# Splitting one 1x1 convolution's third output tile over two banks of the attention buffer

## The chip, the cores and the metric

The kernel runs on one core of a Trainium2 chip. The metric is the time of one execution on the device in microseconds (us), taken as the median of several executions. TensorE (PE in the profile) multiplies matrices, VectorE (DVE) and ScalarE (ACT) work elementwise and empty the matmul results, GpSimd (POOL) does copies, and DMA queues (SP) move data. Matmul results land in PSUM, which is divided into eight banks[...].

## What is computed

The input is eight images of 384 channels and 64x64 pixels. Two layers follow each other, each with a residual:

```python
x = x + L0(gn(x))   # windowed attention: norm, qkv, two branches of 4 heads, 8x8 windows, projection
x = x + L1(gn(x))   # 1x1 conv, a filter on 8x8 patches in the frequency domain,
                    # 3x3 depthwise conv, gate, 1x1 conv:
    x1, x2 = t[:, :192], t[:, 192:]
    g = gelu(x1) * x2
    return einsum('bchw,oc->bohw', g, w_out)
```

The change is in the last line. The weight `w_out` is 384 x 192: the sum runs over 192 gated channels, the result has 384 channels, and the residual is added to it.

## The kernel before

An image is cut into eight strips of eight pixel rows, 512 tokens each. Channels lie on partitions in three tiles of 128. For each image a strip passes through attention, is added to the input and written to DRAM, and is later read back for the second layer.

The work is written as small pieces (`qk_tile`, `scores`, `weights`, `back`, `finish` and so on). Each is given a place on one time line with `at(place, piece, ...)`, and the pieces are emitted in the order of their places. All matmuls and transposes go through the helpers `matmul` (L53) and `transpose` (L56), which keep TensorE's instructions in exactly this order. The order on the other engines is settled by the framework's scheduler when the kernel is built. The second layer of image b runs between the attention pieces of image b+1; only the last image's second layer has no attention beside it.

The eight PSUM banks are dealt out to two pools. `psum` gives one of four single banks (tag "gemm"). `psum2` gives one of two double banks (tag "att"), used in turn by the attention pieces: `scores` writes pS, `turn` pT, `apply` pA, `put` po. In the last image's second layer `conv_taps` uses them too (pc). A buffer is handed to the next tile only when the last reader of the tile before it is done.

The readers that matter here are on VectorE. `normalise` reads pA with a reciprocal (L483) and one multiplication of 128x768 (L484); `weights` reads pS with additions of the position bias (L436). The depthwise convolution's taps (L653) are on VectorE too; their first operand zz comes from ScalarE (L647), which works on the strip that ScalarE has just copied out of pz (L609, L612).

The order on TensorE at one `finish`, by the places in the plan (in units of one attention branch), is: `back` of the newest strip (place 1.99 of its cycle), `apply` of the previous branch (1.00), `scores` of the new branch (0.05), `finish` (0.10), the first `qk_tile` of the next branch (0.14), `put` of the previous branch (0.23). `normalise` has place 0.07 of the same unit, but it is VectorE's.

`finish` (its additions are L686) is the last 1x1 convolution of one strip. Its 192 input channels are a full tile g0 of 128 and a tile g1 that holds the other 64 channels twice: both halves of g1's partitions carry the same 64 channels, so that either half of the array can take them. For each of three output tiles pw there are one 128x128 matmul with g0 and two 64x64 matmuls with g1, each over 512 tokens. A 64x64 matmul occupies a quarter of the array, named by the half of its input partitions (`r`) and the half of its output partitions (`half`). There are 64 calls of `finish`: 8 images by 8 strips.

## Time and profile before

The median of three runs is 3776.54 us (3773.02 to 3777.32). The profiled execution took 3771.3 us.

| engine | busy us | share of the span |
|---|---|---|
| TensorE matmul (PE) | 3639.9 | 97% |
| TensorE weight loads (PEld) | 2315.5 | 61% |
| VectorE (DVE) | 2839.3 | 75% |
| ScalarE (ACT) | 2379.7 | 63% |
| GpSimd (POOL) | 438.2 | 12% |

TensorE's granted clock is 0.997 of full speed over the run. The span falls into three parts: loading and preparing up to about 590 us, then image after image with both layers beside each other up to about 3525 us, then the last image's second layer alone.

An fp32 matmul appears in the trace as two records, one for each pass: the 64 x 6 small matmuls of `finish` are 768 records, its 64 x 3 full ones 384. A group's line gives the line, engine, operation, output and inputs, the shape, how many records, their busy time together, the mean duration of one, and the idle time of the engine before them. Matmuls overlap in the pipeline, so the distance between the starts of two records says more than the duration of one.

### The profile page before, as it was taken

What the parts mean: (1) busy time and instruction counts of PE and PEld (TensorE: products, weight loads), DVE (VectorE), ACT (ScalarE), POOL (GpSimd) and SP (SyncE); (2) the same over time, 40 slices, a digit from 0 to 9 for tenths busy, and PEclk for the clock granted to TensorE, in tenths of its full rate; (3) what the DMA queues carried; (4) which work ended last, traced back from release to release, by engine and by line L of the source; (5) the groups of instructions that cost most, each with busy time, mean ns of one, the idle gap of its engine ahead of it and who ended that gap; (6) DMA issues with size and microseconds to landing.
All of it is one profiled execution on the core that took longest, in us unless ns stands there. A gap on an engine that the chain in (4) does not pass through costs nothing.

```text
span 3771.3 us, 88216 instructions
## 1 busy us (share of the span) xinstructions
PE 3639.9 (97%) x38144; PEld 2315.5 (61%) x38144; DVE 2839.3 (75%) x4601; ACT 2379.7 (63%) x3946; POOL 438.2 (12%) x776
## 2 busy tenths in 40 slices
PE   4999999999999999999999999999999999999898
PEld 2666666666666666666666656666666666666554
DVE  4554578777877687777887778877788777777898
ACT  1767676666676576665766756666676666676442
POOL 5111111111101011101101011111011111100000
PEclk9999999999999999999999999999999999999999
DMA  4222222323322233323332322322232222221422
GB/s 120 85 82 74 90 99 99 107 88 108 123 97 82 88 132 107 116 79 115 108 113 83 115 96 99 132 79 99 93 127 99 107 88 82 99 79 71 160 101 76
DMA packets 144488, 377.03 MB, mean 100 GB/s; under 512 B 12308, under 2 KB 12900, under 8 KB 144100
## 3 DMA queue, kind: packets, MB, share of 16 engines
q1 hardware_dynamic: 139952, 370.60, 27.9%
q8 instruction: 300, 4.92, 0.5%
q0 software_dynamic: 2048, 0.15, 0.1%
q10 hardware_dynamic: 2100, 0.63, 0.1%
q14 instruction: 88, 0.72, 0.1%
HBM read 270.54 MB, written 100.79 MB: 98 GB/s over the span
## 4 chain that ended last, share of the span: by engine, by line
PE 86%; DVE 5%; ACT 4%; issue 2%; DMA 2%; POOL 0%; ACTq 0%; DVEq 0%; POOLq 0%
PE pq L53 24%; PE pr L53 13%; PE pt L53 13%; PE pvv L53 12%; PE pw L53 6%; PE pS L53 3%; PE pA L53 3%; PE pz L53 3%; PE pT L56 3%; PE po L56 3%; DVE zz L653 2%; PE pf L53 2%; PE ln L53 2%; PE pc L53 1%; DMA rs<-line 1%
## 5 line engine op out<-in xcount | busy, mean ns | idle before, releaser
L653 DVE SCALAR_TENSOR_TENSOR zz<-z,dw_sb,zz 128x512 f32<-128x512 f32 x1490 | 1106.5, 761 | 189.3 <-ACT zz L647 166.5
L53 PE MATMUL pq<-y,wqk_sb 128*128 128x512 f32 x2160 | 990.3, 596 | 0.1
L53 PEld LDWEIGHTS pq<-y,wqk_sb 128*128 128x128 f32 x2160 | 402.8, 190 | 456.5 <-issue 424.7
L53 PE MATMUL pt<-wi_sb,xn 128*128 128x384 f32 x1536 | 535.2, 486 | 7.2 <-DVE x_finish L686 7.2
L53 PE MATMUL pr<-oT,wp_sb 128*128 128x512 f32 x1152 | 523.1, 592 | 1.0 <-DVE oT L517 1.0
L53 PE MATMUL pvv<-wv_sb,y 128*128 128x192 f32 x2880 | 496.0, 326 | 0.1
L53 PEld LDWEIGHTS pvv<-wv_sb,y 128*128 128x128 f32 x2880 | 471.6, 190 | 36.7 <-issue 23.4
L374 ACT ACTIVATE qab<-pq,bq_sb,cst 96x512 f32<-96x512 f32 (+1 forms) x256 | 198.0, 773 | 398.8 <-PE pq L53 397.1
L53 PEld LDWEIGHTS pt<-wi_sb,xn 128*128 128x128 f32 x1536 | 286.1, 190 | 212.9 <-issue 48.6
L374 ACT ACTIVATE kcd<-pq,vec 32x512 f32<-32x512 f32 x512 | 348.9, 681 | 9.0
L53 PEld LDWEIGHTS pr<-oT,wp_sb 128*128 128x128 f32 x1152 | 211.1, 190 | 224.4 <-issue 211.6
L356 POOL COPY y<-y 128x384 f32<-128x384 f32 x112 | 100.2, 895 | 1608.0 <-PE pvv L53 1108.2
L329 DVE TENSOR_TENSOR lr<-m 128x128 f32<-128x128 f32 x64 | 19.7, 308 | 318.3 <-ACT m L327 318.3
L647 ACT ACTIVATE zz<-z,dw_sb 128x512 f32<-128x512 f32 x183 | 133.9, 733 | 192.5 <-PE pw L53 187.0
L315 POOL TENSOR_TENSOR sq<-sq 128x512 f32<-128x512 f32 x128 | 167.4, 1308 | 634.3 <-ACT sq L313 629.3
L374 ACT ACTIVATE qcd<-pq,bq_sb,cst 96x512 f32<-96x512 f32 (+1 forms) x256 | 197.3, 771 | 43.9 <-PE pq L53 40.6
L526 DVE SCALAR_TENSOR_TENSOR x_add<-pr,vec,x_add 128x512 f32<-128x512 f32 x192 | 143.6, 748 | 105.6 <-PE pr L53 103.8
L564 ACT COPY t<-pt 128x384 f32<-128x384 f32 x256 | 124.9, 488 | 147.8 <-PE pt L53 145.0
L408 ACT COPY v<-pvv 128x384 f32<-128x384 f32 x256 | 121.2, 480 | 130.5 <-PE pvv L53 130.0
L53 PE MATMUL pw<-zz,wo_sb 128*128 128x512 f32 x384 | 181.9, 610 | 0.0
L374 ACT ACTIVATE kab<-pq,vec 96x512 f32<-96x512 f32 (+1 forms) x256 | 174.4, 681 | 9.0 <-PE pq L53 7.4
L449 ACT ACTIVATE e<-e 128x1024 f32<-128x1024 f32 x128 | 135.3, 1057 | 53.4 <-DVE e L443 52.0
(139 smaller groups left out, 5273.0 us busy)
## 6 DMA issues: line engine op xcount, KB each, us to landing
x_add<-in_x_dram SPq DMA_DIRECT2D x64, 768.0 KB
x1d<-x_add SPq DMA_DIRECT2D x64, 768.0 KB
x_mix<-x1d SPq DMA_DIRECT2D x64, 768.0 KB
x_finish<-x1d SPq DMA_DIRECT2D x64, 768.0 KB
out_dram<-x_finish SPq DMA_DIRECT2D x64, 768.0 KB
x_norm<-in_x_dram SPq DMA_DIRECT2D x61, 768.0 KB
x_stats<-in_x_dram SPq DMA_DIRECT2D x56, 768.0 KB
rs<-line SPq DMA_DIRECT2D x62, 256.0 KB
```

Of the source, the lines that this page charges most:

```text
L53: tc.keep_in_program_order(nc.tensor.matmul(*args, **kw))
L56: tc.keep_in_program_order(nc.tensor.transpose(*args, **kw))
L315: nc.gpsimd.tensor_tensor(sq[:, 0, :], sq[:, 0, :], sq[:, k, :], ALU.add)
L329: nc.vector.tensor_tensor(rc, m[:, 0:P], m[:, 0:P], ALU.mult)
L356: nc.gpsimd.tensor_copy(dst[:, :, :, :, 0:4], src[:, :, :, :, 4:8])
L374: return nc.scalar.activation(dst[to:to + n], pq[of:of + n], AF.Identity, bias=bias[of:of + n], scale=scale)
L408: nc.scalar.copy(v[:, 2 * g:2 * g + 2, :, 0:HD], pvv[:, 0:384].rearrange("p (g h d) -> p g h d", g=2, h=4))
L449: nc.scalar.activation(e, e, AF.Exp)
L526: nc.vector.scalar_tensor_tensor(t[:, m, :], pr, bp_sb[:, m:m + 1], t[:, m, :], ALU.add, ALU.add)
L564: nc.scalar.copy(t1, pt[:, 0:C])
L647: nc.scalar.activation(zz.rearrange("p (r c) -> p r c", c=SW), z[:, 1:9, 1:SW + 1], AF.Copy, scale=dw_sb[:, m, 4:5])
L653: i = nc.vector.scalar_tensor_tensor(acc.rearrange("p (r c) -> p r c", c=SW), z[:, dy:dy + 8, dx:dx + SW], dw_sb[:, m, TAPS[tap]:TAPS[tap] ...
```

## The change

Before, the third output tile had its two small matmuls in two of the four quarters, over 512 tokens each. The change cuts this tile by tokens into two halves of 256 and gives it a double bank of the attention pool in place of a single bank: tokens 0 to 255 in the first bank, 256 to 511 in the second. The first half's two small matmuls read input rows 0 to 63, the second half's read rows 64 to 127, so that the four small matmuls of 256 tokens lie in all four quarters. The full matmul of this tile is also cut in two, all small matmuls come ahead of all full ones as before, and the three additions to the residual follow all four full matmuls in the program; the third reads both banks in one instruction.

```diff
-        pw = [psum(f"pw_{b}_{s}_{m}") for m in range(KC)]
-
-        for m, half, r in ((0, 0, 0), (1, 1, 1), (0, 1, 0), (1, 0, 1), (2, 0, 0), (2, 1, 1)):
+        pw = [psum(f"pw_{b}_{s}_{m}") for m in range(2)]
+        pw2 = psum2(f"pw2_{b}_{s}")
+        full, lo, hi = slice(0, ST), slice(0, 256), slice(256, ST)
+        pw = [(pw[0], 0, full), (pw[1], 1, full), (pw2[:, 0, lo], 2, lo), (pw2[:, 1, lo], 2, hi)]
+
+        for i, half, r in ((0, 0, 0), (1, 1, 1), (0, 1, 0), (1, 0, 1), (2, 0, 0), (3, 1, 1), (2, 1, 0), (3, 0, 1)):
+            p, m, tok = pw[i]
             rows, cols = slice(r * 64, (r + 1) * 64), slice(half * 64, (half + 1) * 64)
-            matmul(pw[m][cols], wo_sb[rows, 1, m * P + half * 64:m * P + half * 64 + 64], g1[rows],
+            matmul(p[cols], wo_sb[rows, 1, m * P + half * 64:m * P + half * 64 + 64], g1[rows, tok],
                    start=True, stop=False)
-        for m in range(KC):
-            matmul(pw[m], wo_sb[:, 0, m * P:(m + 1) * P], g0, start=False, stop=True)
-            zs["added"] = nc.vector.tensor_tensor(t[:, m, :], pw[m], t[:, m, :], ALU.add)
+        for p, m, tok in pw:
+            matmul(p, wo_sb[:, 0, m * P:(m + 1) * P], g0[:, tok], start=False, stop=True)
+        for m in range(2):
+            nc.vector.tensor_tensor(t[:, m, :], pw[m][0], t[:, m, :], ALU.add)
+        by_half = t[:, 2, :].rearrange("p (o n) -> p o n", o=2)
+        zs["added"] = nc.vector.tensor_tensor(by_half, pw2[:, :, lo], by_half, ALU.add)
```

## The prediction

> **What bounds the kernel now.** I read the page first. Matmuls are busy for 97% of the span, and the chain that ended last is 86% TensorE's:

> ```profile
> PE 3639.9 (97%) x38144; PEld 2315.5 (61%) x38144; DVE 2839.3 (75%) x4601; ACT 2379.7 (63%) x3946; POOL 438.2 (12%) x776
> ...
> PE 86%; DVE 5%; ACT 4%; issue 2%; DMA 2%; POOL 0%; ACTq 0%; DVEq 0%; POOLq 0%
> ```

> So TensorE's time is nearly the kernel's: a column saved there is time saved, and a wait put into its queue is time lost. The view by stretches gives TensorE 2886.8 us busy in the 2935 us from 590 to 3525 us, thus 48 us idle. The waits of TensorE in that stretch:

> ```profile
> PE pS L53 <- issue: 18.3, 25, 2.0
> PE pT L56 <- ACT e L449: 8.1, 8, 1.5
> PE pt L53 <- DVE x_finish L686: 7.2, 6, 1.4
> PE pz L53 <- ACT v L408: 6.6, 12, 1.0
> PE pA L53 <- issue: 6.2, 8, 2.7
> ```

> (columns: total us, times, longest). None is for pA's reader, the multiplication on L484: TensorE never waits for `normalise` now. The groups that the change touches, over the whole run (records, busy us, mean ns of one | idle before):

> ```profile
> L53 PE MATMUL pw<-zz,wo_sb 128*128 128x512 f32 x384 | 181.9, 610 | 0.0
> ...
> L53 PE MATMUL pw<-g,wo_sb 64*64 64x512 f32 x768 | 130.7, 606 | 6.6 <-DVE g L668 5.1 <-issue 1.4
> ```

> Then I read the timeline around single calls of `finish`. This one, at 1106 us, is typical (start, duration, engine, line, operands, count):

> ```profile
> 1105.22 0.22 PE L53 MATMUL pA<-v,eT 64*64 64x49 f32 x1
> ...
> 1105.68 1.54 DVE L653 SCALAR_TENSOR_TENSOR zz<-z,dw_sb,zz 128x512 f32<-128x512 f32 x2 [3.79 <-ACT zz L647]
> ...
> 1106.16 0.59 PE L53 MATMUL pw<-g,wo_sb 64*64 64x512 f32 x1
> ...
> 1106.17 1.94 PE L53 MATMUL pw<-g,wo_sb 64*64 64x512 f32 x11
> ...
> 1107.14 0.25 DVE L483 RECIPROCAL rc<-pA 128x16 f32<-128x16 f32 x1
> 1107.31 0.70 DVE L653 SCALAR_TENSOR_TENSOR zz<-z,dw_sb,zz 128x512 f32<-128x512 f32 x1
> 1107.92 0.95 DVE L484 TENSOR_TENSOR o<-pA,rc 128x768 f32<-128x768 f32 x1
> 1108.03 2.84 PE L53 MATMUL pw<-zz,wo_sb 128*128 128x512 f32 x6
> ...
> 1109.45 0.68 DVE L436 TENSOR_TENSOR e<-pS,bias 128x512 f32<-128x512 f32 x1
> ...
> 1110.05 0.68 DVE L436 TENSOR_TENSOR e<-pS,bias_odd 128x512 f32<-128x512 f32 x1
> ```

> The reader is to see three things. TensorE goes from pA's last matmul straight through pS to pw. VectorE frees pA only at 1107.92 + 0.95 = 1108.87, after three taps (L653), of which the first was held up by ScalarE's zz (3.79 us idle). pS is freed later still, at 1110.73. At the moment of `finish` both double banks are thus in use.

> [...] the four small matmuls of the first two tiles (eight records) take 0.861 us together, and so do the two of the third tile (four records). [...] the third tile's two matmuls come from different rows into one bank, and start 7 to 140 ns apart. [...] `normalise` stands behind taps that wait for ScalarE.

> **The change, part by part.**

> *Columns removed.* Single records start 429 ns apart at 512 columns, 323 at 384 and 163 at 192, so about 0.84 ns a column and some 216 ns at 256. The third tile's small matmuls take two passes of 429 ns = 0.86 us now, and would take 2 x 0.216 = 0.43 us with all quarters filled. **Saved: 0.43 us a call.** The full matmul cut in two is 4 records of 216 ns for 2 of 429, 6 ns more: nothing. Its additional weight load of 190 ns lies beside passes of 216 ns, as the loads of pvv (190 ns, passes of 163 ns) already do. The 64 calls save 27.5 us at most: 52 of them lie beside attention, where TensorE sets the pace (22.4 us), and 12 in the last image's stretch. There, from 3525 to 3771 us, VectorE is busy for 215 us and TensorE for 219 of 246, so I count half of 5.2, 2.6 us. **Together 25.0 us.**

> *Additions.* Three of 681 ns stay three with as many elements. They now follow the fourth full matmul in the program, but VectorE already does them later than that (1111.31 at the call above, when the full matmuls had ended at about 1110.7), so this costs nothing.

> *The single bank set free.* One of four, sooner. The 7.2 us that pt waits for the additions (L686) should go.

> *The wait added.* pw2 takes a double bank in the middle of pA, pS, po. The one that comes free first is pA's. So the fifth small matmul must wait for L484, whose result TensorE needs only at `put` today, after the full matmuls and a `qk_tile`. Queued behind it on TensorE is everything: the full matmuls, for which ScalarE's zz (L647) and VectorE's additions wait, the `qk_tile`, whose copies ScalarE makes, then po and pT. I worked the wait out for every call beside attention from the timeline: TensorE would be at the third tile 0.861 us after the first small matmul; the bank is free at the end of L484, plus 0.055 us, which is what TensorE takes to start after VectorE's end where it waits for L686 today. For the call shown: 1108.87 + 0.055 - 1107.08 = 1.85 us. Seven calls of the 52 lose nothing, the typical one 1.2 to 1.9, eighteen over 2.1 and the worst 3.9 us. **The sum is 86.4 us**, 1.66 us a call. The bank is free 3.4 us after pA's last matmul (median; 1.3 to 5.9), and TensorE wants it after 1.7 us. The 53rd call, at 3521 us, finds no pS beside it and takes another bank. In the last image's stretch pc is read (3622.9 us) well before the next but one asks (3628 us), so no wait is added.

> *What is taken back.* Where TensorE is held up, the others get ahead of it. pT's wait for the exponentials (8.1 us) and pt's for the additions (7.2) are small lags of VectorE and ScalarE; I take 12 of these 15.3 us as absorbed (bounds 0 and 15.3). po would take pS's bank in place of pA's; L436 ended 0.5 to 4 us before po started in the calls that I read, and po comes later than before. No cost.

> *Sum:* 3776.5 - 25.0 + 86.4 - 12 = **3826 us**, 1.3% slower.

> **The rivals.**

> 1. *The wait in full, nothing absorbed* (chance 0.15). The idle time of TensorE stays as it is, and the last stretch gains nothing: 3776.5 + 86.4 - 22.4 = 3841. For it: most idle time of TensorE is put down to "issue" and not to a lag. Against it: the added waits give every other engine time.
> 2. *The long waits shrink* (0.20). The eighteen calls over 2.1 us are those in which the first tap waited longest for ScalarE. With TensorE held back about 1.2 us net at each call, ScalarE may be less late; if no call waits for more than 1.85 us, the sum is 63.2 us, and the time 3776.5 - 25.0 + 63.2 - 12 = 3803. Against it: ScalarE's lateness grows inside one cycle from pz on, and pz moves with TensorE.
> 3. *No wait: faster* (0.15). VectorE's order is settled anew when the kernel is built. If `normalise` stood ahead of the taps, it would end 1.3 us after pA (the least in the trace), and TensorE asks no sooner than 1.54 us after it. The time would be 3776.5 - 25.0 = 3751. For it: seven calls are free already. Against it: the change gives `normalise` no earlier place, and in the calls around 1106 us the taps fill exactly the time in which pA isn't ready.
> 4. *Half of it* (0.08): some calls reordered, about 3776.5 - 25 + 43 - 12 = 3783.

> **How the numbers follow.** My forecast has 0.42, and its time is the prediction. The cases at 3803, 3826 and 3841 together have 0.77; with the half case 0.85. The range from 3776 to 3848 holds these and leaves out the fast one. Within 0.2% of before (3769 to 3784) lies about half of the half case and a little of the fast one: 0.06. Faster 0.14, slower 0.80.

> **What would show it.** In the profile after: a wait "pw <- DVE o L484" as TensorE's largest, some 45 times and 60 to 90 us; the group pw<-g with 64x256 records at about 216 ns apart, busy time of all pw<-g down by some 25 us; L484 still behind two or three L653; pt's wait for L686 gone, pT's smaller. I would be wrong if L484 stood directly behind pA in VectorE's order, if the third tile's matmuls started at once after the fourth, or if ScalarE's zz (L647), which waits for pw today (187 us), set off a new wait of TensorE behind it.

## The result, and the profile after

The changed kernel takes 3866.09 us (3865.25 to 3868.92), against 3776.81 before: a ratio of 1.024, 95% interval 1.0227 to 1.0253. It is 89 us slower; the forecast was 50 us slower, and the range ended 18 us too low. The profiled execution took 3864.6 us, 93.3 more than before.

Busy time and chain of the page of the changed kernel (the same two lines as shown of before, and the clock's line; each of its digits is the granted TensorE clock in tenths of full speed, 9 for 90% or more, in one of 40 slices):

```profile
PE 3660.4 (95%) x38528; PEld 2353.6 (61%) x38528; DVE 2846.7 (74%) x4601; ACT 2380.4 (62%) x3946; POOL 437.9 (11%) x776
...
PEclk9999999999999999999999999999999999999999
...
PE 65%; DVE 17%; ACT 9%; DMA 5%; issue 3%; POOL 0%; ACTq 0%; DVEq 0%; POOLq 0%; SPq 0%
```

The clock's line shows nothing: a slice is 97 us, too coarse for what follows. The chain that ended last has gone over in part from TensorE (86% before, 65% now) to VectorE and ScalarE (9% before, 26% now): it now runs through the convolution's taps and ScalarE's copies. What connects them with TensorE is the first line of TensorE's waits in the stretch beside attention, 590 to 3610 us:

```profile
PE pw L53 <- DVE o L484: 76.7, 40, 3.7
PE pS L53 <- issue: 19.6, 26, 2.2
PE pz L53 <- ACT v L408: 6.7, 12, 1.0
PE pT L56 <- ACT e L449: 6.3, 6, 1.2
PE pvv L53 <- ACT kcd L374: 5.9, 7, 1.2
```

(Columns: total us, times, longest.) The first line is new. pt's wait for the additions (7.2 us before) is gone, pT's has shrunk from 8.1 to 6.3, and a wait of pvv for kcd has come in. The groups of pw over the whole run, from the page, which takes records of 512 and 256 columns together, and then the small matmuls of 256 columns by themselves:

```profile
L53 PE MATMUL pw<-zz,wo_sb 128*128 128x512 f32 (+1 forms) x512 | 207.7, 554 | 0.0
...
L53 PE MATMUL pw<-g,wo_sb 64*64 64x512 f32 (+1 forms) x1024 | 121.7, 520 | 84.2 <-DVE o L484 76.7
...
L53 PE MATMUL pw<-g,wo_sb 64*64 64x256 f32 x512 | 49.2, 428 | 76.9 <-DVE o L484 76.7
```

The small matmuls cost 121.7 us busy, 9.0 less than before, where the prediction looked for some 25; the full ones 207.7, where before they cost 181.9 for just as many columns. These 25.8 us more for the same columns are what the prediction had no term for. One call shows both effects. This is the timeline of TensorE alone:

```profile
2410.36 1.21 PE L53 MATMUL pw<-g,wo_sb 64*64 64x512 f32 x8 [0.68 <-issue]
2414.44 0.66 PE L53 MATMUL pw<-g,wo_sb 64*64 64x256 f32 x8 [2.88 <-DVE o L484]
2415.03 4.54 PE L53 MATMUL pw<-zz,wo_sb 128*128 128x512 f32 x8
2419.41 1.02 PE L53 MATMUL pq<-y,wqk_sb 128*128 128x512 f32 x2
```

and this the table by stretches (the stretch and its length in us, the busy time of PE, PEld, DVE, ACT and POOL, the granted clock, and the DMA's share and GB/s):

```profile
2405.00:2414.50 9.50, 5.95 (x241) 4.78 (x241) 5.59 (x10) 4.81 (x12) 2.61 (x3) 1.00 0.01 2
2414.50:2420.00 5.50, 5.50 (x18) 3.01 (x19) 3.99 (x7) 0.39 (x1) 0.00 (x0) 0.69 0.01 3
2420.00:2430.00 10.00, 10.00 (x34) 5.42 (x33) 9.63 (x18) 8.02 (x16) 0.00 (x0) 1.00 0.75 258
```

After 2.88 us of idle time the small matmuls start at once and at full speed, but the eight full records then take 4.54 us in place of the 2.85 they take elsewhere: the granted clock of that stretch is 0.69. In the records of the granted clock it is exactly 0.5 for 3.413 us, from 2415.9 us on, and full records of 512 columns start 853 ns apart there, where they start 429 ns apart at full clock. Over the whole run the clock is halved for 102.5 us, before for 28.6 us. Beside attention, between 600 and 2950 us, there are fifteen such stretches, 64.9 us together, which at half the rate cost up to half of that, 32 us; before there was none.

From the starts of the records, the change of each part of the 64 calls, after minus before:

| part of `finish` | us |
|---|---|
| from the first small matmul to the third tile's first | +89.6 |
| the third tile's small matmuls, up to the first full one | -21.8 |
| the full matmuls, up to the next work of TensorE | +27.2 |
| sum | +95.0 |

That is the whole of the 93.3 us: all the rest of the kernel together became 1.7 us shorter, though single groups moved by up to 8 us either way.

### The profile page after: what moved, and what is told of

Read it like the earlier page. It is cut to its first block, busy times and chain, and to the rows that moved or that the text cites. A ratio compares the mean times of both kernels' runs of the same rounds, so it can differ in the third digit from the quotient of the medians.

```text
span 3864.6 us, 88984 instructions
## 1 busy us (share of the span) xinstructions
PE 3660.4 (95%) x38528; PEld 2353.6 (61%) x38528; DVE 2846.7 (74%) x4601; ACT 2380.4 (62%) x3946; POOL 437.9 (11%) x776
## 3 DMA queue, kind: packets, MB, share of 16 engines
q1 hardware_dynamic: 139952, 370.60, 27.2%
## 4 chain that ended last, share of the span: by engine, by line
PE 65%; DVE 17%; ACT 9%; DMA 5%; issue 3%; POOL 0%; ACTq 0%; DVEq 0%; POOLq 0%; SPq 0%
PE pq L53 19%; PE pt L53 10%; PE pvv L53 10%; PE pr L53 9%; DVE zz L653 8%; PE pw L53 5%; DMA rs<-line 2%; PE po L56 2%; PE pT L56 2%; PE ln L53 2%; ACT z L609 2%; PE pS L53 1%; PE pz L53 1%; PE pA L53 1%; DMA line<-lr 1%
## 5 line engine op out<-in xcount | busy, mean ns | idle before, releaser
L653 DVE SCALAR_TENSOR_TENSOR zz<-z,dw_sb,zz 128x512 f32<-128x512 f32 x1490 | 1107.0, 761 | 191.1 <-ACT zz L647 167.8
L53 PE MATMUL pq<-y,wqk_sb 128*128 128x512 f32 x2160 | 990.4, 596 | 0.4 <-issue 0.4
L53 PEld LDWEIGHTS pq<-y,wqk_sb 128*128 128x128 f32 x2160 | 403.3, 190 | 437.8 <-issue 403.6
L53 PE MATMUL pt<-wi_sb,xn 128*128 128x384 f32 x1536 | 534.6, 486 | 0.0
L53 PE MATMUL pr<-oT,wp_sb 128*128 128x512 f32 x1152 | 523.1, 593 | 0.9 <-DVE oT L517 0.9
L53 PE MATMUL pvv<-wv_sb,y 128*128 128x192 f32 x2880 | 497.2, 327 | 5.9 <-ACT kcd L374 5.9
L53 PEld LDWEIGHTS pvv<-wv_sb,y 128*128 128x128 f32 x2880 | 471.2, 190 | 45.2 <-issue 22.7
L53 PEld LDWEIGHTS pt<-wi_sb,xn 128*128 128x128 f32 x1536 | 286.3, 190 | 200.7 <-issue 47.6
L53 PEld LDWEIGHTS pr<-oT,wp_sb 128*128 128x128 f32 x1152 | 211.2, 190 | 224.2 <-issue 211.2
L647 ACT ACTIVATE zz<-z,dw_sb 128x512 f32<-128x512 f32 x183 | 133.9, 733 | 290.1 <-PE pw L53 284.6
L53 PE MATMUL pw<-zz,wo_sb 128*128 128x512 f32 (+1 forms) x512 | 207.7, 554 | 0.0
L408 ACT COPY v<-pvv 128x384 f32<-128x384 f32 x256 | 120.9, 478 | 136.6 <-PE pvv L53 134.8
L53 PE MATMUL pw<-g,wo_sb 64*64 64x512 f32 (+1 forms) x1024 | 121.7, 520 | 84.2 <-DVE o L484 76.7
```

Source lines behind the costliest of these rows:

```text
L53: tc.keep_in_program_order(nc.tensor.matmul(*args, **kw))
L408: nc.scalar.copy(v[:, 2 * g:2 * g + 2, :, 0:HD], pvv[:, 0:384].rearrange("p (g h d) -> p g h d", g=2, h=4))
L647: nc.scalar.activation(zz.rearrange("p (r c) -> p r c", c=SW), z[:, 1:9, 1:SW + 1], AF.Copy, scale=dw_sb[:, m, 4:5])
L653: i = nc.vector.scalar_tensor_tensor(acc.rearrange("p (r c) -> p r c", c=SW), z[:, dy:dy + 8, dx:dx + SW], dw_sb[:, m, TAPS[tap]:TAPS[tap] ...
```

## The experiments

The theory was that TensorE waits for `normalise` to free pA's double bank, and that the clock falls after long waits. Its main rival was that the cut into 256 columns is itself slow (twice as many full matmuls and weight loads for the third tile).

**The third tile whole, in a bank of the attention pool.** The kernel before, with one line changed:

```diff
-        pw = [psum(f"pw_{b}_{s}_{m}") for m in range(KC)]
+        pw = [psum(f"pw_{b}_{s}_{m}") for m in range(2)] + [psum2(f"pw2_{b}_{s}")[:, 0]]
```

> The matmuls of before (third tile whole, two small matmuls of 512 tokens, full matmuls and additions in before's order), only the third tile's bank comes from the attention pool. Theory 1 (the wait for pA's bank, and the halved TensorE clock that follows a long wait, make the loss): wait on L484 about 77 us as in the changed kernel, half-clock time about 100 us, and without the 0.43 us a call that the packing saves about 3866 + 25 = 3891 us. Rival 2 (the cut into 256 columns makes the loss, by twice as many full matmuls and weight loads): about 3777 us.

Measured: 3888.87 us, ratio 1.0299 (1.0283 to 1.0314), half-clock time 105 us. The largest wait, and the full matmuls, which are not cut here:

```profile
PE pw L53 <- DVE o L484: 75.6, 40, 3.7
...
L53 PE MATMUL pw<-zz,wo_sb 128*128 128x512 f32 x384 | 206.4, 679 | 0.0
```

So the pool from which the bank comes makes the whole loss without any split, and the split gives back 23 us of it. The same 384 records that cost 181.9 us before cost 206.4 here, so the slower full matmuls do not come from the cut either. The rival falls.

**The third tile split, in two single banks.**

```diff
-        pw2 = psum2(f"pw2_{b}_{s}")
+        pw2 = [psum(f"pw2_{b}_{s}_{o}") for o in range(2)]
...
+        for o, tok in enumerate((lo, hi)):
+            zs["added"] = nc.vector.tensor_tensor(t[:, 2, tok], pw2[o][:, lo], t[:, 2, tok], ALU.add)
```

> The third tile split as in the change, but its two halves in two single banks, and so two additions of 256 in place of one of 2 x 256. Theory 1: no wait on L484. The split alone would give 3777 - 25 = 3752 us; but finish now holds all four single banks, so the next qk_tile must wait for the first addition (L686), which comes some 1 to 2 us after the full matmuls: up to 52 x 1.5 = 78 us as a new wait pq <- x_finish, so 3752 to 3830 us, at full clock unless these waits get long. Rival 2: about 3866 us with no such wait.

Measured: 3903.53 us, ratio 1.0337 (1.0321 to 1.0352), outside what was expected. The kind of wait was right:

```profile
PE pq L53 <- DVE x_finish L692: 95.3, 49, 3.7
```

It was larger than the 78 us allowed for (1.9 us a time), and the half-clock time is 102 us here too, where I had counted on full clock. 3777 - 25 + 95 + (102 - 29) / 2 = 3884. The last 20 us are the saving itself, which is nearly lost: by the starts of records the third tile's small matmuls take 64.2 us up to the first full one, against 66.5 before and 43.8 in the version without waits (the last experiment). Here the fourth single bank can be one that pz held: in 16 calls TensorE stands idle between these matmuls until ScalarE has copied pz (L609 and L612; 9.5 us idle, and more by the starts). There is no free bank in the other pool either: with four single banks in `finish`, the next `qk_tile` waits for the first addition.

**The full matmuls of the first two tiles inside the wait.**

```diff
             p, m, tok = pw[i]
+            if (i, half) == (2, 0):
+                for j in range(2):
+                    matmul(pw[j][0], wo_sb[:, 0, j * P:(j + 1) * P], g0, start=False, stop=True)
...
-        for p, m, tok in pw:
+        for p, m, tok in pw[2:]:
```

> As the changed kernel, but the full matmuls of the first two tiles run before the small ones of the third: 1.72 us of work inside the wait. Theory 1: of the 86 us worked out from before, 26 us are longer than 1.73 us and remain; half-clock time falls below 30 us[...]; two more changes between packed and full matmuls cost about 0.1 us a call, 6 us: 3777 - 25 + 26 + 6 = 3784 us, up to 3795. Rival 2: as the changed kernel, 3866 us.

Measured: 3793.30 us, ratio 1.0045 (1.0028 to 1.0062); half-clock time 37 us, where less than 30 was expected. The wait:

```profile
PE pw L53 <- DVE o L484: 17.0, 16, 1.8
```

73 us of the loss go by order alone, with the same instructions and the same banks. Of this 60 us are wait and at most (102.5 - 37.5) / 2 = 33 us clock, less what the two additional changes between packed and full matmuls cost in each call: by the starts of records the next one begins after 523 and 519 ns where it is 429 between matmuls of one kind, thus 12 us for the 64 calls.

**Useless work inside the wait.**

```diff
+        quads = ((0, 0, 0), (1, 1, 1), (0, 1, 0), (1, 0, 1))
+        for i, half, r in quads * (2 if b < B - 1 else 0):
+            rows = slice(r * 64, (r + 1) * 64)
+            matmul(pw[i][0][half * 64:half * 64 + 64], wo_sb[rows, 1, i * P + half * 64:i * P + half * 64 + 64],
+                   g1[rows], start=True, stop=True)
```

> Work added for nothing: the four small matmuls of the first two tiles run three times in place of once while TensorE would wait (1.72 us more, in all images but the last; each repeat overwrites the one before). Theory 1a (long idle stretches of TensorE halve its clock, and this costs some 35 to 40 us of the loss): the wait falls to about 26 us, half-clock time from 103 us to below 40, and the added work beyond the wait (30 + 7 us) is about paid back: 3860 to 3880 us. Theory 1b (the lowered clock is no cause, the loss is all waiting): 3866 + 37 = 3903 us.

Measured: 3874.90 us, ratio 1.0263 (1.0247 to 1.0278). The two groups that answer, of this kernel (the first from the page):

```profile
L53 PE MATMUL pw<-zz,wo_sb 128*128 128x512 f32 (+1 forms) x512 | 183.9, 503 | 0.0
...
L53 PE MATMUL pw<-g,wo_sb 64*64 64x256 f32 x512 | 46.9, 387 | 19.8 <-DVE o L484 19.5
```

The full matmuls are down from 207.7 to 183.9 us busy, although nothing was done to them. 56 x 1.72 = 96 us of work were added. By the starts of records the third tile's delay fell by 65 us (the idle time before it by 76.7 - 19.5 = 57 us) and the time of the full matmuls by 24 us. 96 - 65 - 24 = 7 us, and 9 us were measured. Half-clock time fell to 45.2 us (less than 40 was expected), by 57 us, which is worth up to 29 us. Without the clock's part the kernel would have been at 3866 + 96 - 65 = 3897. This is what shows that idle time of TensorE costs more than its length.

**Finish at a later place, in the changed kernel and in the kernel before.** Only the place in the plan differs:

```diff
-            at(u + 6.10, finish, b, s)
+            at(u + 6.20, finish, b, s)
```

For the changed kernel:

> The changed kernel with finish at place 6.20 in place of 6.10, so that it follows the next qk_tile (2.58 us of matmuls) and pA is normalised when pw2 asks for its bank. Theory 1: of the wait, 11 us remain (what is over 2.58 us), the clock stays full, the packing saves 25 us: 3777 - 25 + 11 = 3763 us. If the move itself costs something, the next kernel shows it. Rival 2 (the split itself is slow): 3866 us.

For the kernel before:

> Control: the kernel before with the same later place of finish. Theory 1: the bank wait has no part here, so no gain: 3777 us within 10. If it gains as the one above does, the place and not the bank is the cause.

Measured: 3776.41 us for the changed kernel (ratio 0.9998, 0.9989 to 1.0007), and 3833.96 us for the kernel before (1.0145, 1.0129 to 1.0160). The first says that 90 us of loss vanish when a `qk_tile` runs while `normalise` works: the wait is 3.1 us in all. It misses the expected 3763 by 13 us. By the starts of records pq's share of TensorE's time is 13.6 us longer and pS's last matmuls' 12.2 us longer than before. At the later place TensorE goes from packed matmuls (pS) to full ones (pq), back to packed ones (pw) and to full ones again, two changes more than before. The same starts price them: pq follows pS after 0.15 us, where pw followed it after 0.03, and pw follows pq after 0.52 us in place of 0.43. That is 0.21 us a call and 11 us for the 52 calls; the other 15 us of the two groups are not traced. I had expected the control to be neutral, and it was not. In TensorE's waits from 590 to 3560 us:

```profile
PE pq L53 <- DVE x_finish L686: 24.5, 20, 2.1
```

With three single banks in `finish` and the next `qk_tile` already holding one, the following one must wait for the additions. At this place the change is worth 57 us. About 23 of them are the split, if it gives here what it gave at the earlier place; the rest is most likely the relief of the pool of single banks, in which the control waits. The same change loses 89 us at one place and gains 57 at another.

**Normalise ahead of the taps.** The changed kernel, with an ordering edge on VectorE and no new wait between engines:

```diff
-        nc.vector.tensor_tensor(
+        zs["normed"] = nc.vector.tensor_tensor(
...
+        if b < B - 1 and tap == 1:
+            behind(i, zs["normed"], mybir.DependencyClass.NoSync, "normalise first")
```

> The changed kernel with an ordering edge on VectorE: the first tap of each convolution tile stands behind the latest normalise (L484), so that no taps stand before it. The bank is then free 1.3 us after pA's last matmul, TensorE asks for it 1.54 us after or later. Theory 1: no wait, full clock, 3777 - 25 = 3752 us, plus what the taps' later start costs, up to 10 us. Rival 2: 3866 us.

The kernel before with the same edge:

> Control: the kernel before with the same ordering edge. Nothing of TensorE waits for normalise there, so 3777 us within 10; a gain here would belong to the order and not to the bank.

Measured: 3759.25 us for the changed kernel (ratio 0.9950, 0.9935 to 0.9965) and 3778.12 us for the kernel before (1.0002, 0.9993 to 1.0010). The timeline of the first kernel around the call that the prediction showed:

```profile
1103.46 0.22 PE L53 MATMUL pA<-v,eT 64*64 64x49 f32 x1
...
1103.76 0.26 DVE L483 RECIPROCAL rc<-pA 128x16 f32<-128x16 f32 x1 [3.33 <-PE pA L53]
...
1104.05 0.96 DVE L484 TENSOR_TENSOR o<-pA,rc 128x768 f32<-128x768 f32 x1
...
1104.93 1.53 DVE L653 SCALAR_TENSOR_TENSOR zz<-z,dw_sb,zz 128x512 f32<-128x512 f32 x2
1105.09 0.59 PE L53 MATMUL pw<-g,wo_sb 64*64 64x512 f32 x1
...
1105.15 1.47 PE L53 MATMUL pw<-g,wo_sb 64*64 64x512 f32 x15
...
1106.54 2.85 PE L53 MATMUL pw<-zz,wo_sb 128*128 128x512 f32 x8
```

L484 ends at 1105.01, 1.3 us after pA and just before `finish` begins. The sixteen small records run without a break, and the full ones at 2.85 us. The wait of pw for L484 is 0.4 us in the whole run. With this edge the change does what it was meant for: 3759 against 3778 us with the same edge and no split, 19 us. It is the one version that beats both kernels.

## Why the prediction was wrong

The order on VectorE around one call of the changed kernel, and the third tile's start on TensorE:

```profile
1125.81 0.75 DVE L653 SCALAR_TENSOR_TENSOR zz<-z,dw_sb,zz 128x512 f32<-128x512 f32 x1
...
1126.48 0.25 DVE L483 RECIPROCAL rc<-pA 128x16 f32<-128x16 f32 x1
...
1126.65 0.70 DVE L653 SCALAR_TENSOR_TENSOR zz<-z,dw_sb,zz 128x512 f32<-128x512 f32 x1
...
1127.27 0.95 DVE L484 TENSOR_TENSOR o<-pA,rc 128x768 f32<-128x768 f32 x1
...
1128.36 0.66 PE L53 MATMUL pw<-g,wo_sb 64*64 64x256 f32 x8 [0.64 <-DVE o L484]
```

- *The direction and its cause were right.* TensorE's largest wait is "pw <- DVE o L484", 40 times, 76.7 us; the forecast was some 45 times and 60 to 90. VectorE's order stayed as it was, with taps ahead of the reciprocal and one between it and L484, so rivals 3 and 4 fell. Rival 2 fell too: the waits did not shrink, several are longer than worked out (4.0 us against 3.9 at most).
- *The size of the wait was right.* 86.4 us were worked out from the trace of before, 89.6 us is what the third tile starts later. (The 86.4 us count from the third tile's own starts in the trace, as the call shown does with 1107.08; counted from 0.861 us after the first small matmul, as the text says, they are 89.4.)
- *The saving was a little too high.* The prediction had 25.0 us. In the version without waits the third tile's small matmuls, up to the first full one, take 22.7 us less than before (66.5 to 43.8). In most calls of the changed kernel beside attention the prediction's 0.43 us a call is 0.36: the way from the tile's first small record to the first full one, taken as 0.86 us, was 0.955 before and is 0.592. The last small record starts 0.29 us after the first, where it was 0.44, and not half of that; from there on it is 0.31 us in place of 0.52, as the columns would have it.
- *The step that failed is the price of a wait, taken as its length alone.* No term stood for the clock. Half-clock time grew from 28.6 to 102.5 us, which costs at most half of the difference, 37 us. By the starts of records the full matmuls take 27.2 us more, of which the version without waits keeps 2.4; about 25 us are the clock's. The clock granted in such a stretch is 0.5, and eleven of the fifteen gaps that came with one beside attention were shorter than 3.413 us, the shortest such stretch, down to 1.7 us. I had read waits of 2 to 3.9 us in the trace and looked only at their sum.
- *"What is taken back" was too large as well.* I took 12 us of other waits as absorbed. pt's 7.2 us went, pT's fell by 1.8 and pA's for instructions by 3.4, but pvv's new wait for kcd (5.9 us) and a longer one of pS (1.3) stand against it. All waits of TensorE beside attention but the one for L484 fell from 47.8 to 43.0 us, by 4.8.

With the measured parts: 3776.5 - 22.7 + 89.6 + 27.2 = 3871, against 3866 measured; the two profiled executions differ by 93.3 us, the medians by 89. Rival 1, which absorbed nothing, came nearest with 3841 and lacked the clock like the rest.

## What to carry to other kernels

A buffer of a pool in rotation is paid for when the reader of the tile before it has not finished: look up in the trace when that reader ends and when the new writer would ask, call by call, before counting what the new shape saves. Where TensorE sets the pace, look at the granted clock behind the waits as well as at their lengths: in the changed kernel 15 of the 26 waits over 1.9 us beside attention came with a stretch at half clock, and the full matmuls of the 64 calls took about 25 us more for it. Here an edge that moved the reader up took away nearly all of both (0.4 us of wait), and useful work moved into the gap most of both (17.0 us of wait). Change the order of the reader's engine together with the buffer: neither the change (89 us slower) nor the edge (no difference) was worth anything alone, together they gave 0.5%.
